# Moving the border offsets out of the one-hot rounds of a token-sorting kernel, with its work lists laid out anew

## The chip, the cores and the metric

The kernel runs on one core of a Trainium2 chip. The time is that of one execution on the device, in microseconds (us); the median of several runs is given. The engines are named as in the profile: PE (TensorE's matmuls), PEld (its weight loads), DVE (VectorE), ACT (ScalarE), POOL (GpSimd) and SP (SyncE, which here only issues transfers).

## The reference

8192 tokens (16 sequences of 512) of 512 features in fp32. Each token gets six vectors of 512, weighed by a softmax `w` of six numbers; a two-layer MLP with a layer norm maps their concatenation back, and the input is added:

```python
h = _ln(x, pw_g[pathway_ids], pw_b[pathway_ids])
h = _ln(h, cp_g[compartment_ids], cp_b[compartment_ids])
t = _ln(x, tm_g[time_steps], tm_b[time_steps])
m = x + _mlp_ln(memory_state, ...)[:, None, :]      # n, r alike
s = _ln(x, ms_g[scale_type], ms_b[scale_type])
cat = jnp.concatenate([w[0] * h, w[1] * t, w[2] * m, w[3] * n, w[4] * r, w[5] * s], axis=-1)
out = x + _mlp_ln(cat, int_W1, int_b1, int_W2, int_b2, int_g, int_be)
```

`_mlp_ln` is `silu(s @ W1 + b1) @ W2 + b2`, normalised. `compartment_ids` and `time_steps` are one list of five values; `scale_type` has the values of a mask. So a token's group, its pair (time step, scale), fixes the tables by which `t` and `s` are scaled, and scaling can be folded into the weights of layer 1 for tokens that are sorted by group.

## The kernel before

**Sorting (up to about 36 us).** The kernel sorts the 8192 tokens by group and sequence. With places counted, it must move token numbers to their new place, and it does so with one-hot matrices: 64 columns in 8 rounds of U = 8 (`one_hots`, L874 to L892). In each round DVE compares for `rows_` (L879) and for m of the 8 columns of `cols_`; ScalarE makes the other columns by a Square and a Relu each (L888, L889); PE adds the 8 products into `pn` (L892). Three buffers take turns, so round k waits for the products of round k - 3. `m` is 6 or 5 by turns.

Between the rounds the loop at L1032 puts small steps on the borders between groups: `place_borders`, `count_rows` and `count_ends` after rounds 0, 1 and 3, and after round 4 `row_places`: two products into `poff` on PE, two copies of it by ScalarE (`off` L945, `total` L946), and two comparisons by POOL (`past`, L948). After the rounds `wx_` is scaled (L1036), and `row_pairs` (L1019) makes three sums of products, `pgc`, of which the third comes from `past`. Ahead of the rounds PE does the first layer of the three conditioning MLPs, `ph`.

**Tiles.** The sorted tokens are worked on in 16 tiles of 512 tokens, each of 4 row groups of 128. A tile's work is cut into some 200 pieces, named by letters, a tile (`p` the previous, `c` the current, `n` the next, `m` the next but one) and a number. Three lists of such names set the order in which all engines' instructions are issued: `ORDER` (startup: conditioning, tables, tile 0, parts of tile 1, extra rows), `WINDOW` (run 15 times with w = 0 to 14) and `LAST`. Within an engine instructions run in this order, and semaphores join the engines. The pieces needed below:

- on PE: `lX`, `lV`, `lH` (`layer1`, L404), `m7` (`half_product`, L452, a half product of layer 1), `q7` (`seventh`, L546, one of seven products by which layer 2 is made, into `pq_0a`, `pq_0b`, `pq_1a`, `pq_1b`);
- layer 1 to layer 2: `ha` adds (DVE, L472), `hs` is the Silu (ScalarE, L475), `tz` turns 32 x 32 blocks (DVE, L197), `sZ` spreads them (transfers issued by SP, `catZ<-rZ`), `zs` makes the sums that the seven products need (POOL, L532 to L538);
- layer 2 out: `kb` puts the bias into a `pq` (ScalarE, L520), `kf` copies a first part (ScalarE, L556, L558), `sf` adds the second to it (DVE, L565), `ku` and `sl` the last ones; `lq` (ScalarE, L612) and `lv` (DVE) make the sums of squares, `lp` the power of them (POOL, L625), `lb` scales, `po` puts out;
- `sp` and `bd` (ScalarE L257, DVE L265) build the scaled weights `vs` of a row group, and run only where the group has a new segment (`if_new`);
- `fs`, `fp`, `fn` (statistics, their power on POOL, norm), `gc`, `gh`, `ga`, `gx`, `gt` (gathers by POOL), and for the conditioning `cs`, `cp` (power on POOL, L1283), `cn`, `ct` (`pt`, PE, L1295).

## Time and profile before

| what | us |
|---|---|
| three runs, lowest / median / highest | 917.75 / 918.54 / 918.93 |
| the profiled execution | 922.05 |
| its span in the profile | 920.3 |

The profiled execution is one execution of its own and longer than the median; its span is 1.75 us shorter than its time, which is what lies around the span.

| engine | busy us | share of the span |
|---|---|---|
| PE | 887.0 | 96% |
| DVE | 726.6 | 79% |
| POOL | 669.5 | 73% |
| ACT | 520.4 | 57% |

A share is a mean over stages. Where the engine with the most work is idle, and what it then waits for, is read stage by stage: from the busy time of every stretch, from the list of its waits, and then from the timeline around a wait, in which a bracket behind an instruction gives the idle time of its engine before it and what ended it.

### The profile page before, as it was taken

The numbers are of one execution on the slowest core, as the hardware profiler recorded it, in microseconds if no ns is written. First come the engines' busy times: TensorE is split into PE (matmuls) and PEld (weight loads), VectorE is DVE, ScalarE is ACT, GpSimd is POOL, SyncE is SP. The second block draws the span as 40 slices with busy tenths as digits, with TensorE's granted clock in tenths as the row PEclk, the third lists the DMA queues.
The fourth block names the chain that finished last, engine by engine and source line by source line (L and its number), as shares of the span: only waits on it lengthen the run. The fifth ranks groups of instructions, "written<-read, shape, count | busy, mean of one in ns | idle before, by whom it ended". The sixth has DMA issues, their size and how long they took to land. (4 is left out here: it accounts for less than half of the span.)

```text
span 920.3 us, 13553 instructions
## 1 busy us (share of the span) xinstructions
PE 887.0 (96%) x3617; PEld 642.2 (70%) x3617; DVE 726.6 (79%) x1360; ACT 520.4 (57%) x1261; POOL 669.5 (73%) x730
## 2 busy tenths in 40 slices
PE   6989899999999999999999999999998999999995
PEld 6744346868686877768686868777685867778682
DVE  8687776868787798968787878869697888879565
ACT  4669835464655648374646556574757466573413
POOL 9777778577778678686868687867767777876452
PEclk9989999999999999999999999999999999999998
DMA  8757686777777777777778686777666776776513
GB/s 273 231 183 228 201 251 186 192 230 197 228 187 233 196 218 192 208 206 208 230 199 222 196 234 183 234 204 214 180 190 198 202 226 187 228 195 192 148 41 111
DMA packets 88557, 185.40 MB, mean 201 GB/s; under 512 B 24324, under 2 KB 24388, under 8 KB 88476
## 3 DMA queue, kind: packets, MB, share of 16 engines
q0 software_dynamic: 31104, 104.88, 40.0%
q1 hardware_dynamic: 56668, 79.53, 29.6%
q8 instruction: 30, 0.49, 0.2%
q14 instruction: 51, 0.42, 0.2%
q10 hardware_dynamic: 704, 0.08, 0.1%
HBM read 100.48 MB, written 19.97 MB: 131 GB/s over the span
## 5 line engine op out<-in xcount | busy, mean ns | idle before, releaser
L404 PE MATMUL p<-vs,catV 128*128 128x512 f32 x512 | 228.1, 593 | 4.0 <-DVE vs L265 1.7
L404 PEld LDWEIGHTS p<-vs,catV 128*128 128x128 f32 x512 | 96.6, 190 | 108.4 <-issue 100.8
L452 PE MATMUL p<-wh__81,catH 128*128 128x256 f32 x480 | 110.9, 379 | 0.0
L452 PEld LDWEIGHTS p<-wh__81,catH 128*128 128x128 f32 x480 | 91.2, 190 | 12.4
L638 POOL DMA_INDIRECT out<-yb,tok x64 | 76.9, 1201 | 31.3 <-issue 15.1
L376 ACT ACTIVATE pw<-pw,rsh 128x512 f32<-128x512 f32 x64 | 45.6, 714 | 92.9 <-DVE pw L383 53.7
L475 ACT ACTIVATE add<-add 128x512 f32<-128x512 f32 x64 | 39.6, 625 | 91.8 <-DVE add L472 72.2
L350 ACT ACTIVATE junk<-pw 128x512 bf16<-128x512 f32 x60 | 37.6, 626 | 88.2 <-DVE pw L347 39.1
L171 POOL DMA_INDIRECT cp<-cp_rows,i_cp x64 | 74.4, 1162 | 14.5 <-issue 12.8
L625 POOL TENSOR_TENSOR rsy<-vey,mhalf 128x4 f32<-128x4 f32 (+1 forms) x16 | 23.6, 1474 | 83.1 <-DVE veh L368 70.1
L391 POOL TENSOR_TENSOR xbs<-xbs,rows 128x512 f32<-128x512 f32 x64 | 82.2, 1286 | 1.3
L171 POOL DMA_INDIRECT xbs<-in_x,tok x64 | 66.0, 1031 | 22.0 <-issue 18.2
L171 POOL DMA_INDIRECT pw<-in_pw,i_pw x64 | 63.0, 984 | 25.1 <-issue 12.2
L171 POOL DMA_INDIRECT add<-rows,i_add x64 | 66.9, 1045 | 19.3 <-issue 19.3
L383 DVE SCALAR_TENSOR_TENSOR pw<-pw,sumsh,cp 128x512 f32<-128x512 f32 x60 | 45.6, 761 | 39.7 <-DMA cp<-cp_rows,i_cp 31.2
L317 ACT ACTIVATE xm<-xbs,nmx,rsx 128x512 f32<-128x512 f32 x64 | 49.0, 807 | 26.9 <-DVE nmx L311 12.5
L372 POOL TENSOR_TENSOR rsh<-veh,mhalf 128x1 f32<-128x1 f32 x64 | 48.5, 758 | 14.9 <-DVE veh L368 11.6
L452 PE MATMUL p<-wt,catH 128*128 128x256 f32 x240 | 56.7, 379 | 0.0
L452 PE MATMUL u<-wt,catX 128*128 128x256 f32 x240 | 56.6, 379 | 0.0
L346 DVE SCALAR_TENSOR_TENSOR pw<-xbs,sums,pw 128x512 f32<-128x512 f32 x60 | 46.0, 767 | 12.5 <-DMA pw<-in_pw,i_pw 6.8
L452 PE MATMUL u<-wx__80,ss 128*128 128x256 f32 x240 | 54.5, 379 | 0.0
L452 PEld LDWEIGHTS u<-wx__80,catX 128*128 128x128 f32 x240 | 45.6, 190 | 12.7 <-issue 6.9
(439 smaller groups left out, 2131.2 us busy)
## 6 DMA issues: line engine op xcount, KB each, us to landing
catX<-rX SPq DMA_DIRECT2D x240, 64.0 KB
catV<-rV SPq DMA_DIRECT2D x240, 64.0 KB
catZ<-rZ SPq DMA_DIRECT2D x240, 64.0 KB
catH<-rH SPq DMA_DIRECT2D x240, 64.0 KB
rows<-adde SPq DMA_DIRECT2D x8, 256.0 KB
yb<-in_int_W SPq DMA_DIRECT2D x1, 1024.0 KB
catH<-in_int_W SPq DMA_DIRECT2D x1, 1024.0 KB
w1x<-in_int_W SPq DMA_DIRECT2D x1, 1024.0 KB
```

The lines of the kernel that those rows point to most:

```text
L171: nc.gpsimd.indirect_dma_start(dst, None, table, bass.IndirectOffsetOnAxis(ap=idx, axis=0), **kw)
L317: nc.scalar.activation(t, st["xb"][:, j, :], AF.Identity, bias=st["nm"][:, j : j + 1], scale=st["rs"][:, j : j + 1])
L346: nc.vector.scalar_tensor_tensor(h, st["xb"][:, j, :], st["sums"][:, 1, j : j + 1], h, ALU.add, ALU.mult)
L350: nc.scalar.activation(junk, x, AF.Identity, accum_out=sums[:, 0, k : k + 1])
L372: nc.gpsimd.tensor_tensor(rs, st.pop(("ve", j)), mhalf[:, :1], ALU.pow)
L376: nc.scalar.mul(pw[:, :D], pw[:, :D], st.pop(("rs", j)))
L383: nc.vector.scalar_tensor_tensor(pw[:, :D], pw[:, :D], st["sh", j][:, 1], cp, ALU.add, ALU.mult)
L391: nc.gpsimd.tensor_add(st["xb"][:, j, :], st["xb"][:, j, :], rows[:, 2, :])
L404: nc.tensor.matmul(st["p1", g], st["c" + blk][:, g, c, :], m[:, c, :], start=(blk == first and c == order[0]), stop=(blk == last and c == ...
L452: nc.tensor.matmul(dst, m[:, c], at_["half1"][k][:, c], start=(k == 1 and c == 0), stop=(c == NC - 1), skip_group_check=True)
L475: nc.scalar.activation(st["add", g], st["add", g], AF.Silu)
L638: nc.gpsimd.indirect_dma_start(out_rows[j], bass.IndirectOffsetOnAxis(ap=tok[:, j, w : w + 1], axis=0), yb[:, j, :], None)
```

## The change

- `row_places` is called behind the eight rounds and not after round 4, and so is `segment_picks`. The two comparisons leave it; they are now `rows_past`, a piece `rp1` of the startup list.
- `row_pairs` makes two sums of products; the third, from `past`, is `rest_rows`, the piece `rp2`, into a buffer `prr` of its own. `past` gets a buffer of its own.
- DVE's number of columns `m` is 5 in five rounds and 6 in three (43 columns, 44 before), ScalarE's 21 (20 before).
- The first layer of the third conditioning MLP (`cond_1(2)`) is issued after round 2 and not ahead of the rounds.
- `ORDER` and `WINDOW` are new; `WINDOW` has the same 197 names. `LAST` is as it was.

```diff
-    for s in range(3):
+    def cond_1(s):
         n = stT[s].shape[1]
...
+    cond_1(0)
+    cond_1(1)
...
-        m = U - 2 - k % 2
+        m = U - 3 + (k % 3 == 2 or k == NQ // U - 1)
...
-    past = [cols[:, n] for n in (3, 4)]
+    past = [t.rearrange("p (v n) -> p v n", v=2)[:, v] for t in (prep.tile([P, 2 * NQ], F32, name="past")[:NB],) for v in range(2)]
...
         nc.scalar.copy(off, poff[:NB, :1])
         nc.scalar.copy(total[:1], poff[:1, 1:2])
+
+    def rows_past():
         for v, i_at in enumerate((i_pos, i_next)):
             pl.tensor_scalar(past[v], i_at[:NB], beg, n_b, ALU.is_gt, ALU.mult)
...
     def row_pairs():
-        pgc = ps.tile([P, 3, Q * NW], F32, tag="p", name="pgc")
+        pgc = ps.tile([P, 2, Q * NW], F32, tag="p", name="pgc")
...
+    def rest_rows():
+        prr = ps.tile([P, Q * NW], F32, tag="p", name="prr")
         for v in range(2):
-            nc.tensor.matmul(pgc[v * NH : (v + 1) * NH, 2], ones[:NB, :NH], past[v], start=True, stop=True)
-        return (pgc,)
+            nc.tensor.matmul(prr[v * NH : (v + 1) * NH], ones[:NB, :NH], past[v], start=True, stop=True)
+        nc.vector.tensor_add(i_rest, i_rest, prr)
...
-        nc.vector.tensor_add(i_rest, i_rest, pgc[:, 2])
...
-        for make in {0: (first_rows, place_borders), 1: (count_rows,), 3: (count_ends,), 4: (row_places, segments, segment_kinds), 6: (segment_picks,)}.get(q0 // U, ()):
+        for make in {0: (first_rows, place_borders), 1: (count_rows,), 3: (count_ends,), 2: (lambda: cond_1(2),), 4: (segments, segment_kinds)}.get(q0 // U, ()):
             make()
+    row_places()
+    segment_picks()
...
-    hs.c.3 bd.n.0 po.p.3
+    m7.c.1.3 sX.n.3
```

**ScalarE in the rounds.** `room` is the scratch of a column, `vs` and `xbs` the buffers of the rounds. Before, around round 4:

```order
L888 ACTIVATE room_118<-room_118,catZ 128x64
L889 ACTIVATE vs_86<-room_118,catZ 128x64
L945 COPY off<-poff 14x1
L946 COPY total<-poff 1x1
L888 ACTIVATE room_118<-room_118,catZ 128x64
L889 ACTIVATE xbs_91<-room_118,catZ 128x64
L888 ACTIVATE room_118<-room_118,catZ 128x64
L889 ACTIVATE xbs_91<-room_118,catZ 128x64
```

After, the last columns and what follows them:

```order
L892 ACTIVATE room_118<-room_118,catZ 128x64
L893 ACTIVATE vs_86<-room_118,catZ 128x64
L892 ACTIVATE room_118<-room_118,catZ 128x64
L893 ACTIVATE vs_86<-room_118,catZ 128x64
L949 COPY off<-poff 14x1
L950 COPY total<-poff 1x1
L1047 ACTIVATE wx__80<-yb,wx 128x2048
```

The copies of `off` and `total` stood between the columns of round 4 and those of round 5, and now stand behind the last column, ahead of `wx_`.

**PE within a window, the second half of layer 2.** `pq_1a` and `pq_1b` are the sums of the second pair of row groups, the `p_` with L404 is `lV.c.2`, and the `p_` with L452 is `m7.c.1.4`. Before:

```order
L546 MATMUL pq_1b<-w_82,catZ 128x256 x2
L546 MATMUL pq_1b<-w2t,zs_5233 128x256 x2
L546 MATMUL pq_1a<-w2t,zs_5233 128x256 x2
L404 MATMUL p_9_2_5306<-vs_85,catV 128x512 x3
L248 UNCONDITIONAL_BRANCH
L404 MATMUL p_9_2_5306<-vs_85,catV 128x512
L248 UNCONDITIONAL_BRANCH
L546 MATMUL pq_1b<-w2t,catZ 128x256 x2
L546 MATMUL pq_1b<-w_82,zs_5233 128x256 x2
```

After:

```order
L546 MATMUL pq_1b<-w2t,zs_5254 128x256 x2
L546 MATMUL pq_1b<-w_82,catZ 128x256 x2
L452 MATMUL p_9_3_5202<-wt_1595,catH 128x256 x4
L546 MATMUL pq_1a<-w2t,zs_5254 128x256 x2
L546 MATMUL pq_1b<-w2t,catZ 128x256
L248 UNCONDITIONAL_BRANCH
L546 MATMUL pq_1b<-w2t,catZ 128x256
L546 MATMUL pq_1b<-w_82,zs_5254 128x256
L248 UNCONDITIONAL_BRANCH
L546 MATMUL pq_1b<-w_82,zs_5254 128x256
L404 MATMUL p_9_2_5329<-vs_85,catV 128x512 x4
```

`lV.c.2` stood ahead of the last two products into `pq_1b` (`q7.p.1.4` and `q7.p.1.3`) and now stands behind them; `m7.c.1.4`, which stood near the end of the window, now stands among them.

**ScalarE at the same place of the window.** L558 with `pq_1b` is `kf.p.3`, L612 is `lq.p.0`, L317 the norm of the next tile's rows. Before:

```order
L520 COPY pq_1b<-rows 128x512
L239 TENSOR_LOAD new_v
L556 COPY yb<-pq_1a 128x256
L317 ACTIVATE xm_1_5311<-xbs_89,nmx,rsx 128x512
L317 ACTIVATE xm_3_5313<-xbs_89,nmx,rsx 128x512
L558 COPY yb<-pq_1b 128x256
L569 COPY yb<-pq_1a 128x256
```

After:

```order
L556 COPY yb<-pq_1a 128x256
L520 COPY pq_1b<-rows 128x512
L317 ACTIVATE xm_1_5314<-xbs_89,nmx,rsx 128x512
L317 ACTIVATE xm_3_5316<-xbs_89,nmx,rsx 128x512
L612 ACTIVATE junk,ssy<-yb 128x512
L558 COPY yb<-pq_1b 128x256
L317 ACTIVATE xm_2_5338<-xbs_89,nmx,rsx 128x512
L317 ACTIVATE xm_0_5340<-xbs_89,nmx,rsx 128x512
L569 COPY yb<-pq_1a 128x256
```

`lq.p.0` now stands ahead of `kf.p.3`; it stood behind it and behind the copy of L569.

## Rows read from the trace of the kernel before

**Rows 1.** The first part of the page.
```profile
span 920.3 us, 13553 instructions
...
PE 887.0 (96%) x3617; PEld 642.2 (70%) x3617; DVE 726.6 (79%) x1360; ACT 520.4 (57%) x1261; POOL 669.5 (73%) x730
```

**Rows 2.** Stretches: length, busy PE, PEld, DVE, ACT, POOL; clock, DMA, GB/s.
```profile
57.00:75.00 18.00, 15.31 (x65) 6.61 (x64) 14.41 (x42) 14.83 (x35) 13.48 (x14) 0.81 0.44 132
...
75.00:165.00 90.00, 85.20 (x253) 44.23 (x252) 63.80 (x117) 59.76 (x134) 68.05 (x67) 1.00 0.74 217
...
165.00:855.00 690.00, 683.01 (x2724) 516.05 (x2723) 568.81 (x1026) 398.42 (x967) 512.82 (x507) 1.00 0.73 207
```

**Rows 3.** Waits of PE: total us, times, longest.
```profile
PE pq_0b L546 <- POOL yb L532: 4.3, 5, 1.6
...
PE p L404 <- DVE vs L265: 1.7, 1, 1.7
```

**Rows 4.** Timeline, 23 to 36 us: start, us, engine, line, work [idle <-releaser].
```profile
23.66 4.02 POOL L948 TENSOR_SCALAR rows<-room,begs,n_b 14x64 f32<-14x64 f32 x2
...
25.11 3.66 PE L892 MATMUL pn<-vs 128*64 128x128 f32 x32
...
28.88 1.52 PE L892 MATMUL pn<-xbs 128*64 128x128 f32 x12
...
28.98 0.15 ACT L945 COPY off<-poff 14x1 f32<-14x1 f32 x1 [4.42 <-PE poff L944]
...
30.68 0.43 PE L892 MATMUL pn<-xbs 128*64 128x128 f32 x2 [0.27 <-ACT xbs L889]
...
31.66 3.87 PE L892 MATMUL pn<-vs 128*64 128x128 f32 x32
...
34.95 1.99 ACT L1036 ACTIVATE wx__80<-yb,wx 128x2048 f32<-128x2048 f32 x1
```

**Rows 5.** Timeline, 57 to 60 us, POOL and PE.
```profile
58.00 0.59 POOL L1283 TENSOR_TENSOR rsc<-vec,mhalf 96x1 f32<-96x1 f32 x1
...
59.48 0.52 PE L1295 MATMUL pt<-ident,room 96*128 96x96 f32 x4 [1.98 <-issue]
```

**Rows 6.** Timeline, 692 to 709 us, ACT, DVE, POOL, PE.
```profile
695.14 2.55 ACT L257 ACTIVATE vs<-ws,scs 128x512 f32<-128x512 f32 x4
...
697.60 0.61 ACT L475 ACTIVATE add<-add 128x512 f32<-128x512 f32 x1
...
698.25 0.71 DVE L197 STREAM_TRANSPOSE rZ<-add 128x512 f32<-128x512 f32 x1 [2.32 <-ACT add L475]
...
708.13 0.73 POOL L532 TENSOR_TENSOR yb<-catZ 128x256 f32<-128x256 f32 x1 [1.75 <-DMA catZ<-rZ]
...
708.91 0.48 PE L546 MATMUL pq_0b<-w2t,yb 128*128 128x256 f32 x1 [1.61 <-POOL yb L532]
```

**Rows 7.** Timeline, 561 to 566 us, ACT, PE, DVE.
```profile
561.58 0.35 ACT L558 COPY yb<-pq_1b 128x256 f32<-128x256 f32 x1
...
561.67 3.60 PE L404 MATMUL p<-vs,catV 128*128 128x512 f32 x8
...
562.70 0.38 DVE L565 TENSOR_TENSOR yb<-yb,pq_1b 128x256 f32<-128x256 f32 x1
...
563.86 0.63 ACT L612 ACTIVATE junk<-yb 128x512 bf16<-128x512 f32 x1
...
564.39 0.19 ACT L612 ACTIVATION_READ_ACCUMULATOR junk<-yb 128x1 f32 x1
...
565.10 1.03 PE L546 MATMUL pq_1b<-w2t,catZ 128*128 128x256 f32 x4
...
565.97 1.03 PE L546 MATMUL pq_1b<-w,zs 128*128 128x256 f32 x4
```

**Rows 8.** The page's costliest groups, L625 on POOL.
```profile
L625 POOL TENSOR_TENSOR rsy<-vey,mhalf 128x4 f32<-128x4 f32 (+1 forms) x16 | 23.6, 1474 | 83.1 <-DVE veh L368 70.1
```

**Rows 9.** Timeline, 642 to 645 us, PE.
```profile
642.84 2.38 PE L404 MATMUL p<-vs,catV 128*128 128x512 f32 x5 [1.70 <-DVE vs L265]
```

73 lines of the change are left out of this document (37 added, 36 removed).

## The prediction

> **What bounds the kernel now.** I read the page's share of busy time first: PE works 887.0 us of a span of 920.3 us [rows 1]. The 33 us left are all that any change of order can win, unless it removes PE work or gives PE a faster clock, so the next thing to see is where they lie. The table by stretches says it [rows 2]: from 165 to 855 us, the steady windows, PE is busy 683.01 of 690 us and idle 7.0; from 75 to 165 it is idle 4.8; from 57 to 75 it is idle 2.7 of 18, and the granted clock there is 0.81, the one stretch of this table in which it is well under 1. The list of PE's waits names most of the windows' idle time [rows 3]: 4.3 us in five waits for POOL's `yb` (the correction that a seventh product of layer 2 reads, L532) and 1.7 us in one for `vs` (L265). These six waits are 6.0 of the 7.0 us.
>
> So a step of the change counts if it shortens PE's work or one of those waits. What it does to ScalarE (57% busy) or POOL (73%) alone costs nothing until PE waits for it.
>
> **The one-hot rounds.** Before, ScalarE stands 4.42 us in the copy of `off`, because the product that it reads is queued on PE behind the 32 matmuls of a round (25.11 us, 3.66 us long) [rows 4]. It is then late with its two columns of the next round: PE idles 0.27 us at 30.68, and the same again (0.28) at 31.39. The 16 matmuls of that half round begin at 28.88 and the next 32 at 31.66, so they take 2.78 us; at the pace of the row at 25.11 (3.66 / 32 = 0.114 us) they would take 1.83. The change puts product and copy behind the last round, so ScalarE isn't held any more: 0.95 us less.
>
> The other edits here. DVE makes 43 columns in place of 44 and ScalarE 21 in place of 20: one more Square and Relu, hidden by the 4.42 us that ScalarE no longer stands. Uncovered it would be two instructions, under 1 us. `cond_1(2)` moves 8 matmuls from ahead of the rounds to behind round 2; the number is the same, so 0. The two products of the third row pair move into a piece of the startup list (`rp2`) with DVE's addition: again the same work, PE's share two short products, 0. POOL's two comparisons (4.02 us at 23.66 [rows 4]) move into the same list behind the table products: POOL is held there in place of here. Queued behind them on POOL are gathers and powers for the extra rows and tile 1, and `rp2` on PE and DVE waits for them; I take 0, since these gathers are issued well ahead of use, and up to +4 if the whole hold reached PE (in the bounds of the next term). `off` is copied ahead of the scaling of `wx_` (34.95), which in before starts before PE's last product of the rounds is done; it now waits for a product queued behind the same matmuls, some 0.6 us later. DVE reads the result of the rounds at the same time, and PE has the products of the cond vectors and tile 0 in its queue, so I take 0. Bounds of the whole term: 0, if DVE's compares and not ScalarE set the pace of rounds 5 to 7, and -2, if the later rounds close up too. Taken: **-0.95**.
>
> **The startup list, behind the rounds.** It is laid out anew in all engines, so its sum is bounded, not added up. The gap of this stretch is one PE wait of 1.98 us, for `pt` at 59.48 [rows 5]. Its operand comes through DVE from POOL's power (L1283), which runs at 58.00, behind gathers of tokens. In the new order the four gathers `gt.0` still stand ahead of `cp`, which comes before `cn` and `ct`: the same chain of the same instructions. So the gap stays, and with it the low clock behind it. Taken: **0**. The bounds: if the gap is closed, the 2.7 us of idle time go and also what the clock takes, (1 - 0.81) x 18 = 3.4 us, together -6.1; if POOL's moved comparisons are uncovered in their new place, +4.
>
> On the clock the row shows this: 0.81 granted in the 18 us in which PE stood 2.7 us, 1.00 in the stretch behind it, in which it was busy 85.2 of 90 [rows 2]. [...]
>
> **The windows.** WINDOW has the same 197 pieces in another order, so PE's busy time stays and only its waits move.
>
> Three of the five `yb` waits are of one kind [rows 6]: ScalarE runs the four `s_part` instructions (L257, 695.14, 2.55 us), needed only when a row group has a new segment, ahead of the last `hidden_silu` (697.60). DVE turns its result at 698.25, SP spreads it, POOL adds at 708.13 after 1.75 us of waiting for that transfer, and PE starts at 708.91 after 1.61 us idle. Two things stand otherwise in the new order: the silu of row group 3 no longer stands behind the whole of the window's last products, since a half product (`m7.c.1.4`; 4 products by the order, which the trace counts as 8 matmuls) is taken out from among them; four of such a size start 0.87 us ahead of the next four (565.10 and 565.97 [rows 7]), so the eight are 1.73 us of PE's time. ScalarE's queue in the next window begins with this silu, then the copies (L520), then L257, in the same order as before. I give the chain 0.55 us of the 1.73, because the silu still waits for DVE's addition and that for the last other products: 3 x 0.55 = 1.65 (bounds 0 and the 4.3 whole).
>
> The other two `yb` waits have POOL late with a power (`fp.c.3`); POOL spends 83.1 us in 16 windows idle ahead of L625 (`lp.p`) [rows 8], 5.2 each, nearly all for DVE's work. The new order issues `gc.n.0` ahead of it, in that idle time, and not between it and the power `fp.n.0`, so what follows on POOL is sooner by about one gather. The two are short, so I take 0.9 off both together (bounds 0 and 4.3 - 1.61 = 2.7).
>
> The wait for `vs`: ScalarE's L257 and then DVE's L265 are late, and PE starts at 642.84 after 1.70 [rows 9]. Same head start: 1.0 (bounds 0 and 1.7).
>
> Against these stands one new tight place. `q7.p.1.4` writes the second `pq_1b` group, and must wait until DVE has added the first (L565), which needs ScalarE's copy of it (L558). Before, PE does the eight products of `lV.c.2` in between (561.67 to 565.10, 3.43 us), and L565 ends at 562.70 + 0.38 = 563.08, 2.0 us ahead of need [rows 7]. In the new order the 3.43 us move behind, `m7.c.1.4` comes in front (1.73), so PE wants `pq_1b` at 561.67 + 1.73 = 563.40, and `lq.p.0` (0.63 at 563.86, and 0.19 for its read-out, 0.82) stands ahead of L558 on ScalarE. The cover falls from 2.0 us to 0.3. In a quiet window that holds; in the five disturbed ones, where DVE and ScalarE run up to a microsecond late, I put 0.2 each: +1.0 (bounds 0 and the second rival below). `kf` and `sf` are behind it on their engines, and the next thing late would be `lV.c.2`.
>
> Windows together: -1.65 - 0.9 - 1.0 + 1.0 = **-2.55**; bounds -6 (all six waits gone) and +6 (0.4 us of new waiting in each of 15 windows). LAST is unchanged: 0.
>
> **Sum.** -0.95 + 0 - 2.55 = -3.5. It is made against the profiled execution, 922.05 us (a span of 920.3 and 1.75 around it): 918.55. The median of the timed runs is 918.54, 3.51 below the profiled one, so the forecast is 918.54 - 3.5 = 915.0.
>
> **The rivals.**
> 1. The gain is eaten. For it: in 57 to 75 us ScalarE is busy 14.83 of 18 us [rows 2], so a start 1 us sooner meets a full engine, and the chain of the silu [rows 6] has SP and a transfer in it that a sooner silu needn't move. Against: the rounds' loss is PE's own. Then 918.54 less 0 to 1: about 918.
> 2. Slower: the wait of `q7.p.1.4` for L565 comes in every window. Its price is 0.3 of missing cover and more when `lq.p.0` (0.82) delays L558 fully, 0.82 - 0.3 = 0.5 to 0.7, say 0.6: 15 x 0.6 = 9.0, so -0.95 - 3.55 + 9.0 = +4.5, 923.0. It decides from (0.95 + 3.55 + 1.84) / 15 = 0.42 us a window. Against it: ScalarE is free 43% of its time [rows 1] and L558 and L565 take 0.73 us together, so part of the 0.82 is taken up.
> 3. The `pt` gap closes after all, because the power comes sooner with fewer pieces between: -6.1 more, 908.9. Against it: four gathers still stand ahead of it on POOL.
>
> **How the numbers follow.** Forecast 0.5 (912 to 917.5), gain eaten 0.2 (917 to 919), slower 0.17 (920 to 926), gap closed 0.13 (906 to 911). Leaving out most of the slower case's upper part and the lowest of the gap case, the range is 908 to 921. What a measurement of this kernel can tell from no change is about 0.2%, 1.84 us, so faster means under 916.7 and slower over 920.4. Faster: 0.13 + 0.9 x 0.5 = 0.58; slower: nearly all of its case, 0.16; the same: the rest, 0.26.
>
> **What would show it.** In the profile after: the copy of `off` with no wait that holds a round, and no idle time of PE in the rounds from 28 to 32; PE's wait for `pt` still near 2 us and a clock of about 0.8 behind it; five or fewer waits of `pq_0b` for `yb` with a sum of 1 to 3 us; a new row "pq_1b waits for DVE" with about 1 us. Wrong it is if that row has 5 us or more, if PE's busy time moves by over 3 us (the clock), or if the startup ends more than 3 us earlier or later: then the list laid out anew decides, which I bounded and did not add up.

## The result: 0.3% slower, and the profile after

The changed kernel takes 923.31 us (median of 16 runs, 920.22 to 926.8). The kernel before, run beside it, takes 920.18 us (16 runs, 917.53 to 922.67). The ratio is 1.0031 with a 95% interval of 1.0016 to 1.0046: slower by 2.9 us, 1.5 to 4.2. The forecast was 915.0, range 908 to 921. It was made on a median of three runs, 918.54; over 16 runs the same kernel has 920.18, so 1.6 us of the distance is the base and the rest the change. One and the same kernel scatters over 5 us between executions; that matters for all that follows.

The profiled execution of the changed kernel took 924.86 us, 2.81 more than that of before, with PE busy 2.8 us longer (page, first part; before in [rows 1]):

```profile
span 922.7 us, 13762 instructions
...
PE 889.8 (96%) x3617; PEld 639.8 (69%) x3617; DVE 724.8 (79%) x1360; ACT 518.6 (56%) x1263; POOL 649.3 (70%) x730
```

The waits of PE over the whole span (total us, times, longest; before in [rows 3]):

```profile
PE pq_1b L546 <- POOL zs L532: 1.8, 1, 1.8
...
PE pq_0b L546 <- POOL yb L532: 1.4, 3, 0.9
...
PE pq_1b L546 <- DVE yb L565: 1.3, 1, 1.3
...
PE p L404 <- DVE vs L265: 0.9, 2, 0.6
```

The waits that the windows were to lose are lower: `yb` 1.4 for 4.3 us, `vs` 0.9 for 1.7. But `zs` and L565 are new, 3.1 us together. The stretches after (start and end, length, busy time of PE, PEld, DVE, ACT and POOL, granted clock, share and GB/s of the transfers; before in [rows 2]):

```profile
36.00:57.00 21.00, 19.94 (x134) 9.38 (x137) 17.82 (x56) 8.17 (x29) 16.82 (x21) 0.75 0.73 237
...
57.00:75.00 18.00, 16.40 (x96) 7.36 (x87) 11.77 (x34) 17.65 (x42) 10.88 (x12) 0.91 0.46 136
...
165.00:855.00 690.00, 683.79 (x2721) 514.44 (x2720) 562.86 (x1023) 395.22 (x965) 492.29 (x507) 1.00 0.72 206
```

Of before, the first of these stretches is not in [rows 2]:

```profile
36.00:57.00 21.00, 21.00 (x198) 10.95 (x197) 15.33 (x53) 12.27 (x36) 15.48 (x20) 0.92 0.76 244
```

From 165 to 855 us PE is busy 683.79 of 690, 0.8 more than before: the windows are even. From the first product of layer 2 to the last first product it is 714.8 us before (148.0 to 862.8) and 714.8 after (150.5 to 865.4). **In these two profiles the 2.4 us by which the span grew are all there at 150 us.** How much of that is the change and how much the two executions is a question that one profile of each can't answer; the table below takes it up.

In the rounds the change did what it says (timeline; start, us, engine, line, work, in brackets the idle time before and what ended it; before in [rows 4]):

```profile
15.56 5.52 PE L896 MATMUL pn<-vs 128*64 128x128 f32 x32 [0.33 <-DVE bi L917]
...
27.29 1.91 PE L896 MATMUL pn<-xbs 128*64 128x128 f32 x16
...
29.12 1.96 PE L896 MATMUL pn<-vs 128*64 128x128 f32 x16
...
31.32 1.96 PE L896 MATMUL pn<-vs 128*64 128x128 f32 x16 [0.24 <-DVE vs L887]
...
33.49 0.15 ACT L949 COPY off<-poff 14x1 f32<-14x1 f32 x1 [4.49 <-PE poff L948]
```

ScalarE still waits 4.49 us for `off`, but nothing of the rounds is queued behind it; the last products run at 1.96 / 16 = 0.123 us each with one wait of 0.24, and the rounds end at 33.28 us in place of 35.52. Behind them this gain no longer shows. The next table has the landmarks of the profiles that have one of the two startup lists unmoved (e6 but for the tables' load): the granted clock from 36 to 60 us, the end of the rounds, PE's first flip of the extra rows (`px`, a transpose by a product with `ident`), the first product of layer 2, and the way between these two. Ratios are to the kernel before, timed on the same chip; those in brackets are of kernels cut short after three windows.

| kernel | lists | clock | rounds end | first flip | layer 2 | flip to layer 2 | ratio |
|---|---|---|---|---|---|---|---|
| before | old | 0.93 | 35.5 | 78.0 | 148.0 | 70.0 | 1 |
| e3_new_window | old startup | 0.72 | 34.6 | 80.0 | 150.8 | 70.9 | 0.9995 |
| e6_tables_last | old | 0.93 | 34.1 | 77.1 | 147.9 | 70.8 | 1.0026 |
| e9_short_before | old | 0.72 | 34.6 | 79.9 | 150.0 | 70.0 | (0.3473) |
| e7_rounds_alone | old, rounds edited | 0.72 | 33.3 | 79.0 | 149.7 | 70.7 | 1.0002 |
| e10_short_rounds | old, rounds edited | 0.86 | 33.4 | 76.2 | 145.8 | 69.5 | (0.3480) |
| e15_rounds_new_window | old startup, rounds edited | 0.72 | 33.4 | 79.2 | 150.6 | 71.4 | 1.0015 |
| e4_new_order | new startup | 0.93 | 35.6 | 79.9 | 152.6 | 72.7 | 1.0009 |
| after | new, rounds edited | 0.72 | 33.3 | 78.0 | 150.5 | 72.6 | 1.0031 |
| e2_old_window | new startup, rounds edited | 1.00 | 33.8 | 77.8 | 149.8 | 72.1 | 1.0015 |
| e14_copy_first | new startup, rounds edited | 0.86 | 33.3 | 78.2 | 150.3 | 72.0 | 1.0020 |
| e11_short_startup | new startup, rounds edited | 0.93 | 33.3 | 76.2 | 149.4 | 73.2 | (0.3498) |

With the startup list of before the last stretch takes 69.5 to 71.4 us in seven profiles, with the new one 72.0 to 73.2 in five; the two do not overlap, whatever the clock did ahead of them. That is not yet a loss: 1.3 us of it is work that the new list puts behind the flip and the old one ahead of it (counted below, under the extra rows' chain). Layer 2 itself begins at 145.8 to 150.8 us with the startup list of before and at 149.4 to 152.6 with the new one, 1.6 us later in the mean, and these ranges overlap. e4's profile is of the longest of its twelve executions (930.01 us).

### The profile page after: what moved, and what is told of

The parts are those of the page before. It is cut to its first block, busy times and chain, and to the rows that moved or that the text cites. A ratio compares the mean times of both kernels' runs of the same rounds, so it can differ in the third digit from the quotient of the medians.

```text
span 922.7 us, 13762 instructions
## 1 busy us (share of the span) xinstructions
PE 889.8 (96%) x3617; PEld 639.8 (69%) x3617; DVE 724.8 (79%) x1360; ACT 518.6 (56%) x1263; POOL 649.3 (70%) x730
## 5 line engine op out<-in xcount | busy, mean ns | idle before, releaser
L404 PE MATMUL p<-vs,catV 128*128 128x512 f32 x512 | 228.3, 593 | 2.8 <-ACTq L248 1.1
L404 PEld LDWEIGHTS p<-vs,catV 128*128 128x128 f32 x512 | 97.0, 190 | 107.2 <-issue 100.4
L452 PE MATMUL p<-wh__81,catH 128*128 128x256 f32 x480 | 111.0, 379 | 0.0
L452 PEld LDWEIGHTS p<-wh__81,catH 128*128 128x128 f32 x480 | 91.4, 190 | 18.2 <-issue 6.7
L171 POOL DMA_INDIRECT pw<-in_pw,i_pw x64 | 67.6, 1057 | 42.4 <-DVE veh L368 27.1
L638 POOL DMA_INDIRECT out<-yb,tok x64 | 66.6, 1040 | 32.4 <-issue 16.4
L171 POOL DMA_INDIRECT xbs<-in_x,tok x64 | 68.2, 1066 | 24.0 <-issue 11.7
L171 POOL DMA_INDIRECT add<-rows,i_add x64 | 69.4, 1084 | 19.9 <-issue 16.2
L171 POOL DMA_INDIRECT cp<-cp_rows,i_cp x64 | 65.4, 1022 | 15.5 <-issue 12.9
L625 POOL TENSOR_TENSOR rsy<-vey,mhalf 128x4 f32<-128x4 f32 (+1 forms) x16 | 19.2, 1202 | 67.6 <-DVE vey L620 67.6
L372 POOL TENSOR_TENSOR rsh<-veh,mhalf 128x1 f32<-128x1 f32 x64 | 44.9, 701 | 30.8 <-DVEq L248 21.6
L317 ACT ACTIVATE xm<-xbs,nmx,rsx 128x512 f32<-128x512 f32 x64 | 48.8, 808 | 21.8 <-DVE nmx L311 21.6
L452 PE MATMUL p<-wt,catH 128*128 128x256 f32 x240 | 56.8, 380 | 0.2 <-DMA catH<-rH 0.2
L452 PE MATMUL u<-wt,catX 128*128 128x256 f32 x240 | 56.6, 380 | 0.1
L452 PE MATMUL u<-wx__80,ss 128*128 128x256 f32 x240 | 54.5, 380 | 0.6 <-DVE veh L368 0.6
L452 PEld LDWEIGHTS u<-wx__80,catX 128*128 128x128 f32 x240 | 45.7, 190 | 12.6 <-issue 3.8
```

What stands on the lines that cost most here:

```text
L171: nc.gpsimd.indirect_dma_start(dst, None, table, bass.IndirectOffsetOnAxis(ap=idx, axis=0), **kw)
L317: nc.scalar.activation(t, st["xb"][:, j, :], AF.Identity, bias=st["nm"][:, j : j + 1], scale=st["rs"][:, j : j + 1])
L372: nc.gpsimd.tensor_tensor(rs, st.pop(("ve", j)), mhalf[:, :1], ALU.pow)
L404: nc.tensor.matmul(st["p1", g], st["c" + blk][:, g, c, :], m[:, c, :], start=(blk == first and c == order[0]), stop=(blk == last and c == ...
L452: nc.tensor.matmul(dst, m[:, c], at_["half1"][k][:, c], start=(k == 1 and c == 0), stop=(c == NC - 1), skip_group_check=True)
L638: nc.gpsimd.indirect_dma_start(out_rows[j], bass.IndirectOffsetOnAxis(ap=tok[:, j, w : w + 1], axis=0), yb[:, j, :], None)
```

## The experiments

### Which of the three parts costs: rounds, startup list, window list

The change has three parts that can be taken apart: the edits of the rounds, `ORDER` and `WINDOW`. Four kernels each had some of them.

**e1_rounds_only**: the edits of the rounds, both lists of before.

```diff
 (before, with all hunks of the change but the two lists)
-    ... nv.e0.2 wh nv.e0.3 ... vv.0.1 ar
+    ... rp1 (13 places ahead of ar) ... vv.0.1 rp2 ar
```

> The kernel before with the edits of the rounds alone: border offsets and copy behind the rounds, 43 and 21 columns, the third conditioning product between the rounds, the third row pair as pieces rp1 (13 places ahead of add_rows in the startup list of before) and rp2 (right ahead of it). Startup list and window list are those of before. Theory A (the rounds gain what the traces show, 35.52 to 33.28 us, and the startup list laid out anew loses it again): last product of the rounds at about 33.3 us, first product of layer 2 (148.0 before) at 146 to 147, time 1.5 to 2.2 us below before, ratio 0.9978. Rival B (startup time is set elsewhere, by clock and transfers, whatever the rounds do): rounds end at 33.3, but layer 2 begins at 148 or later, ratio 1.000.

Measured: 927.94 us, ratio 1.0055 (1.003 to 1.008), above the whole change's ratio, with intervals that meet. The rounds end at 33.4 as expected, the first product of tile 0 comes at 66.9, but layer 2 at 155.7. PE's timeline around the new piece `rp2`:

```profile
79.44 0.48 PE L1035 MATMUL prr<-past,room 14*64 14x64 f32 x4
...
82.90 6.73 PE L404 MATMUL p<-wx__80,catX 128*128 128x512 f32 x8 [2.98 <-ACT catZ L1368]
```

Behind `prr` (L1035) tile 0's third product waits 2.98 us for ScalarE's copy of a flip. All PSUM buffers of this kernel come from one ring of eight (its pool `ps`, bufs=8), so a buffer more shifts every later user onto another predecessor; by the releaser the product here got one that was still being read. The wait is only half of the price: from 78.8 to 89.0 us this execution was granted 0.50, and the product's 8 matmuls took 6.73 us, where they take 3.60 at a granted 1.00 (before, at 78.47; 3.1 more). Wait and clock together, 6.1 us, are about what layer 2 is later than in e7 below (149.7). The old list was made without that buffer. So this run doesn't isolate the rounds; e7 does.

**e2_old_window**, **e3_new_window**, **e4_new_order**: the other combinations.

```diff
 e2 (after):   -WINDOW of after        +WINDOW of before
 e3 (before):  -WINDOW of before       +WINDOW of after
 e4 (before):  -ORDER of before        +ORDER of after, without rp1 and rp2
```

> The changed kernel with the window list of before; rounds and startup list as changed. Theory A (startup list loses 4.7 us, rounds gain 2.2, windows even): layer 2 begins at 150.5 us as in the changed kernel, time 2.5 us over before, ratio 1.0027. Rival C (the window list is what costs): ratio 1.000 or below.

> The kernel before with the new window list alone. Theory A: the windows are even (714.8 us from the first to the last begin of layer 2 in the profile of before, 714.9 in that of the changed kernel), ratio 1.000 with 0.001 either way; waits for yb 1 to 2 us less, the wait for zs or for DVE's L565 1 to 3 us more. Rival C (the window list is what costs): ratio 1.003 or more.

> The kernel before with the new startup list alone (without the pieces rp1 and rp2, which it does not have); rounds and window list as before. Theory A: the rounds end at 35.5 us, layer 2 begins 4 to 5 us later than 148.0, ratio 1.005. Rival B (the startup time is set by clock and transfers, whatever the rounds do): layer 2 begins at about 150.5 as in the changed kernel, ratio 1.0027. Rival C (the window list is what costs): ratio 1.000 or below.

Measured: e2 1.0015 (0.9987 to 1.0042), e3 0.9995 (0.9972 to 1.0019), e4 1.0009 (0.9987 to 1.0031). The window list alone does nothing that can be measured, against rival C, and its waits for `yb` are 2.3 us there; the forecast's -2.55 would be 0.9972, the very end of the interval. The other two lean to the slow side within their intervals; e4's layer 2 at 152.6 us is where theory A had it, its time is not (1.0009 for 1.005). Single runs of a list differ by more than the list: the stretch of the windows was 714.8, 714.6, 710.9 and 718.1 us in four profiles with the old window list (before, e1, e2, e4).

**e7_rounds_alone**: a cleaner form of the rounds, without another PSUM buffer.

```diff
 (before; shortened, without the parts that it shares with the change)
...
-        m = U - 2 - k % 2
+        m = U - 3 + (k % 3 == 2 or k == NQ // U - 1)
...
-    4: (row_places, segments, segment_kinds), 6: (segment_picks,)
+    2: (lambda: cond_1(2),), 4: (rows_past, segments, segment_kinds)
+    row_places(); segment_picks()     # behind the rounds; the third row pair stays in pgc
```

> The kernel before, with both its lists, and of the change only what frees ScalarE in the rounds: offset products, copies and segment_picks behind the rounds, 43 and 21 columns, the third conditioning product after round 2. POOL's comparisons stay after round 4 and the third row pair stays in pgc (in the first run of the rounds the third pair had a PSUM buffer of its own in the old list, and tile 0's third product waited 3.0 us for a buffer). Theory A: rounds end at 33.4 us in place of 35.5, first product of tile 0 at 66 to 67, layer 2 begins at 146.5 to 148, ratio 0.998. Rival B (the startup time is set elsewhere): layer 2 begins at 148 to 151, ratio 1.000.

Measured: 1.0002 (0.9973 to 1.003). The rounds end at 33.3 us and the time is that of before: rival B as far as the interval goes, which is wide enough for the forecast's -0.95 (0.999).

Four profiles with the startup list of before were granted the same clock, 0.72 from 36 to 60 us, and can be set side by side: e3 and e9 without the edit of the rounds, e7 and e15 (below) with it. The rounds end at 34.6 and 34.6 against 33.3 and 33.4 us, the first flip comes at 80.0 and 79.9 against 79.0 and 79.2, layer 2 at 150.8 and 150.0 against 149.7 and 150.6. Of 1.25 us at the end of the rounds 0.85 are left at the flip and 0.25, less than the scatter, at layer 2.

### The startup timed by itself

Since the windows scatter by several us, four kernels were cut short: startup, three windows, the last list (five runs each).

```diff
-    for w in range(NW - 1):
+    for w in range(3):
         run(WINDOW, w)
-    run(LAST, NW - 1)
+    run(LAST, 3)
... (and the two places that ask for the last tile)
```

> The kernel before cut short: after the startup it runs only three windows and then the last list on tile 3; the other twelve tiles are not worked on and their rows of the output are not written. With most of the windows' own scatter out of it, the startup can be timed. Expected from the profile of before: 148.0 to the first layer 2, then 51.7 + 50.0 + 54.6 + 57.5 and 1.75 around the span, about 313.5 us.

> e7_rounds_alone cut short in the same way (old lists, ScalarE freed in the rounds; twelve tiles left out). Theory A (the rounds' 2.2 us reach the end of the startup): 1.5 to 2.2 us below e9_short_before. Rival B (what sets the end of the startup does not start with the rounds): within 0.7 us of it.

> e2_old_window cut short in the same way: rounds and startup list as changed, window list of before (twelve tiles left out). Theory F (the change's 2.9 us are lost in the startup): 2 to 3 us over e9_short_before. Rival G (they are lost in the windows): within 0.7 us of it.

> e11_short_startup with the tables' load lt ahead of lh, cut short in the same way (twelve tiles left out). Theory D (the wait for the tables is what the new startup list loses): 2 us below e11_short_startup. Rival E (something later sets the end, as the full run e5_tables_first had it, with layer 2 at 153.2): within 0.7 us of it, or over it.

Measured: before 320.72 us (319.38 to 321.45), rounds edited 320.61 (317.31 to 322.6), new startup list 322.64 (320.12 to 324.12), with the tables first 321.58 (319.94 to 323.58). As ratios to the full kernel before: 0.3473 (0.3464 to 0.3483), 0.3480 (0.3468 to 0.3491), 0.3498 (0.3488 to 0.3507), 0.3482 (0.3469 to 0.3496). The first was expected at 313.5 us, 7 us too low. The first and the third interval don't meet: rounds and new startup list together are 0.0025 of the full time slower, 2.3 us, most of the change's 2.9, and nothing else differs between these two kernels. The edited rounds with the old lists lie within 0.7 us of before, which points at the startup list, as theory F has it; against the edited rounds alone the intervals meet, though. The full kernels show less of it: 1.4 us in e2 and 0.8 in e4, with intervals that hold 1.

Where in the kernel the 2.3 us arise the traces don't say. In the one profile of each, layer 2 begins at 149.96 us in the short kernel before and at 149.38 with the new list, and what follows takes 167.6 and 169.0 us, with the same lists from there on (169.8 in e10, which has the old lists too).

### The tables behind the big loads

In the changed kernel ScalarE stands 4 us at 50 to 55 us (timeline):

```profile
54.65 0.99 ACT L1250 ACTIVATE room<-room,wx 128x128 f32<-128x128 f32 x3 [4.01 <-DMA room<-in_tm_bT]
...
55.11 1.93 PE L1275 MATMUL pb<-wt,room 128*32 128x512 f32 x8 [0.73 <-ACT room L1250]
...
61.50 0.50 PE L1306 MATMUL pt<-ident,room 96*128 96x96 f32 x4
```

It waits for three small tables (`lt`, moved in packets of 20 and 12 bytes, not of 4 as the expectation of e5 says). The new startup list issues their load behind `lh` (a load of 1 MB) and `lo` on SP's queue: at 43.87 us in place of 37.10. ScalarE's next work is queued behind; from 57 to 75 us it is busy 17.65 of 18 us. PE's `pt` (L1306, L1295 before) no longer waits, but only since PE itself comes 2 us later to it, at 61.50 in place of 59.48 [rows 5]; that alone isn't the list, since e3 and e9 with the old one come to it at 62.1, without a wait too.

```diff
 e5 (after)
-    he.0 eh.2 lh wk.2.1 xe.0 wk.2.0 sz gh.0.0 he.1 g5 lo lt fl.3 ...
+    he.0 eh.2 lt lh wk.2.1 xe.0 wk.2.0 sz gh.0.0 he.1 g5 lo fl.3 ...
 e6 (before)
-    he.2 xt.0.1 lt xs.0.1 ... lh gh.0.0 tt fl.2 xe.0 g5 lo xt.0.2 ...
+    he.2 xt.0.1 xs.0.1 ... lh gh.0.0 fl.2 xe.0 g5 lo lt tt xt.0.2 ...
```

> The changed kernel with one name of its startup list moved: lt (the load of the three small tables, 4-byte pieces) ahead of lh (the 1 MB load of wh_) as it stands in the kernel before; in the changed list it stands behind lh and lo on SP's queue, was issued at 43.87 us (37.10 before), and ScalarE waits 4.01 us for it at 54.65 with sct, catX, the four L257 and the norms queued behind. Theory D (this wait is what makes the new startup list lose the rounds' gain): ScalarE's wait is gone, pt is reached at 58 us in place of 61.5, the first product of tile 0 comes at 66 to 67 in place of 68.9, layer 2 begins at 147 to 149, ratio to the kernel before 0.998 to 1.000. Rival E (something later sets the end of the startup): the wait is gone, but layer 2 begins at 150 to 151 all the same, ratio 1.003.

> The reverse in the kernel before: lt moved behind lh and lo (and tt, its user, behind it). Theory D: ScalarE waits 4 us or more for the tables, the first product of tile 0 comes at 70 in place of 67.9, ratio 1.002 to 1.003. Rival E: the wait appears, but layer 2 begins at 148 to 149, ratio 1.000.

Measured: e5 1.0031 (1.0007 to 1.0054), the changed kernel's own ratio; e6 1.0026 (1.0004 to 1.0048) in time, though its profiled execution was a quick one (918.76 us) with layer 2 at 147.9. In e5 ScalarE has the tables without a wait, and tile 0's first product comes at 66.9 in place of 68.9:

```profile
50.38 0.99 ACT L1250 ACTIVATE room<-room,wx 128x128 f32<-128x128 f32 x3
...
75.69 1.52 ACT L317 ACTIVATE xme<-xbs,nmx,rsx 128x512 f32<-128x512 f32 x2 [2.45 <-POOL rsx L300]
...
77.33 0.63 PE L1361 MATMUL px<-ident,pre 128*128 128x128 f32 x4 [1.89 <-ACT xme L317]
...
79.07 1.09 PE L1361 MATMUL px<-ident,pre 128*128 128x128 f32 x4 [1.11 <-ACT vs L257]
...
79.95 6.08 PE L404 MATMUL p<-wx__80,catX 128*128 128x512 f32 x8
```

But then PE stands 1.89 and 1.11 us ahead of the flips, since their input `xme` is ready at 76 to 77 us as ever: it comes from gathers that POOL issues and that the tables have no part in. Layer 2 began at 153.2. Of that 2.5 us and more are the clock's: this execution was granted 0.50 from 78.1 to 84.9 us, and tile 0's third product took 6.08 us in place of 3.60; e12 lost 1.7 us there in the same way (5.30 us, 0.51 from 79.8 to 83.2). e8 (below) has the same startup list, the same wait of 1.89 us ahead of the flip and 1.00 from 75 to 150 us, and its layer 2 at 150.45 is no sooner than with the tables behind. In e6 the wait came (3.13 us), layer 2 no later than before, yet its time is slower by 0.4 to 4.4 us; no trace here shows why. So theory D isn't borne out by the full kernels: the tables' wait is real and mostly covered. The short one leaves it open: e12's ratio lies midway, 1.5 us under e11's, with intervals that meet.

### The extra rows' chain, 75 to 105 us

The stretch from the first flip to layer 2 that is 2 us longer in the profiles with the new list can be divided at the first product of the extra rows, `pe`. The profiles are those of the table above; times in us, in brackets PE's matmuls:

| startup list | flip to layer 2 | PE busy in it | flip to `pe` | PE busy in it | `pe` to layer 2 |
|---|---|---|---|---|---|
| old, seven profiles | 69.5 to 71.4 | 66.6 to 67.0 (179) | 4.5 to 4.8 | 4.5 to 4.6 | 64.7 to 66.5 |
| new without `rp2` (e4) | 72.7 | 67.6 (183) | 6.4 | 5.0 | 66.4 |
| new, four profiles | 72.0 to 73.2 | 68.2 (187) | 6.6 | 5.5 | 65.4 to 66.6 |

So the difference lies between the flip and `pe`, and half of it there is work: `prr` and four transposes of tile 0 (`ptH`), which the old list has ahead of the flip. The other 1.1 us are two waits. But ahead of the flip PE waits less with the new list, 0.3 to 0.8 us (1.0 in e4), than with the old one, 1.5 in six profiles of seven (0.5 in before). So the landmark compared more work with less, and the waits around the flips are about even: 1.4 to 1.8 us in the four profiles of the new list against 1.5 to 1.7 in the six. ScalarE and PE there in the changed kernel:

```profile
76.33 1.52 ACT L317 ACTIVATE xme<-xbs,nmx,rsx 128x512 f32<-128x512 f32 x2 [1.16 <-POOL rsx L300]
...
77.75 2.54 ACT L257 ACTIVATE vs<-ws,scs 128x512 f32<-128x512 f32 x4
...
77.97 0.63 PE L1361 MATMUL px<-ident,pre 128*128 128x128 f32 x4 [0.77 <-ACT xme L317]
...
79.33 0.63 PE L1361 MATMUL px<-ident,pre 128*128 128x128 f32 x4 [0.74 <-DVE pre L1354]
...
80.82 0.80 ACT L317 ACTIVATE xme<-xbs,nmx,rsx 128x512 f32<-128x512 f32 x1
...
82.75 0.58 ACT L1368 COPY catZ<-px 128x512 f32<-128x512 f32 x1 [0.42 <-ACTq L286]
...
84.57 3.70 PE L1376 MATMUL pe<-ws,catZ 128*128 128x512 f32 x8 [0.33 <-ACT catZ L1368]
```

and ScalarE in e7_rounds_alone, with the startup list of before (its lines are three lower there for the same work):

```profile
77.42 1.52 ACT L317 ACTIVATE xme<-xbs,nmx,rsx 128x512 f32<-128x512 f32 x2
...
79.41 0.81 ACT L317 ACTIVATE xme<-xbs,nmx,rsx 128x512 f32<-128x512 f32 x1 [0.48 <-DMA rows<-rows]
...
82.73 0.56 ACT L1365 COPY catZ<-px 128x512 f32<-128x512 f32 x1
...
85.32 2.56 ACT L257 ACTIVATE vs<-ws,scs 128x512 f32<-128x512 f32 x4 [0.36 <-ACTq L286]
```

The old list has the four L257 of tile 0 behind the norms (L317, `xme`) and the first copy of a flip; the new one has them among the norms. The next kernels moved something there; their expectations take the longer stretch for a loss.

**e13_product_first**, and **e16_short_product**, the same cut short:

```diff
 (after; e16: after with the window list of before, three windows)
-    ... fv.0.1 ey.1 ey.0 xs.e1.1 ro.1 ... gx.1.2 ea.0 lX.0.0 rp2 ...
+    ... fv.0.1 lX.0.0 ey.1 ey.0 xs.e1.1 ro.1 ... gx.1.2 ea.0 rp2 ...
```

> The changed kernel with one product of tile 0 (lX.0.0) moved ahead of the flips of the extra rows ey.1 and ey.0 in the startup list. In every run with the new list the way from the first flip (px) to the first layer 2 takes 72.1 to 73.2 us, in every run with the old list 69.5 to 70.9; in the new one PE waits 1.4 to 1.5 us in the two flips (0.77 and 0.74 in the changed kernel) with only this product behind them. Theory H (the new list asks for the flips before the extra rows are normed): the waits are covered by the product's 3.4 us, first flip to layer 2 takes 69 to 71 us counted from where the product now starts, time 1 to 1.5 us below the changed kernel, ratio to before 1.0015 to 1.002. Rival I (a later chain sets the end, the 1.5 us come back as another wait): ratio 1.003, layer 2 at 150 to 151.

> e11_short_startup (rounds and startup list as changed, window list of before, only three windows; twelve tiles left out) with lX.0.0 ahead of the flips as in e13_product_first. Theory H: 1 to 1.5 us below e11_short_startup, 321.3 us, ratio 0.348 to 0.3485 (e9_short_before 0.3473, e11_short_startup 0.3498). Rival I: ratio 0.3495 or more.

Measured: 1.0043 (1.0018 to 1.0067) and 0.3511 (0.3492 to 0.3529), no gain. The waits of the two flips are gone and come back at the next step, as rival I had it:

```profile
80.29 1.04 PE L1361 MATMUL px<-ident,pre 128*128 128x128 f32 x8
...
82.96 0.58 ACT L1368 COPY catZ<-px 128x512 f32<-128x512 f32 x1 [0.42 <-ACTq L286]
...
84.78 1.55 PE L1376 MATMUL pe<-ws,catZ 128*128 128x512 f32 x3 [2.61 <-ACT catZ L1368]
```

PE waits 2.61 us for the copies of the flips (L1368), which ScalarE makes at about the same time as in the changed kernel (82.96 and 82.75). Layer 2 begins at 152.5 and 151.4.

**e17_scales_later**, and **e18_short_scales**, the same cut short:

```diff
 (after; e18: after with the window list of before, three windows)
-    ... vd.0 nv.e0.0 sp.0.0 fn.0.2 ... fs.0.1 bd.0.0 fv.0.1 ... ez.1 wh gc.0.1 ...
+    ... vd.0 nv.e0.0 fn.0.2 ... fs.0.1 fv.0.1 ... ez.1 sp.0.0 wh gc.0.1 bd.0.0 ...
```

> The changed kernel with one pair of its startup list moved: sp.0.0 (ScalarE's four L257, 2.54 us at 77.75) behind ez.1 and its partner bd.0.0 (DVE's L265, 2.71 us at 81.55) behind gc.0.1, near where the old list has them. In the changed kernel they stand between the norms of the extra rows (xme) and the copies of their flips (catZ, L1368), for which the extra rows' products pe wait; moving a product ahead of the flips only turned their wait into a wait of pe for that copy (2.6 us in e13_product_first). Theory L (the extra rows' chain over ScalarE sets the pace from 75 to 105 us, and these four instructions lengthen it): the copies come 2 us sooner, pe begins at 82 to 83 in place of 84.6, layer 2 at 148 to 149, time 1 to 2 us below the changed kernel, ratio 1.001 to 1.002. Rival M (the gathers of the extra rows set the pace): layer 2 at 150 to 151, ratio 1.003.

> e11_short_startup (rounds and startup list as changed, window list of before, only three windows; twelve tiles left out) with sp.0.0 and bd.0.0 later as in e17_scales_later. Theory L: 1 to 2 us below e11_short_startup, ratio 0.348 to 0.3485 (e9_short_before 0.3473, e11_short_startup 0.3498). Rival M: ratio 0.3495 or more.

Measured: 1.0029 (1.0002 to 1.0055) in full, 0.3480 (0.346 to 0.35) cut short. The traces do a part of what theory L says:

```profile
78.59 0.63 PE L1361 MATMUL px<-ident,pre 128*128 128x128 f32 x4 [1.11 <-DVE pre L1354]
...
79.26 0.59 ACT L1368 COPY catZ<-px 128x512 f32<-128x512 f32 x1 [0.50 <-PE px L1361]
...
80.92 2.56 ACT L257 ACTIVATE vs<-ws,scs 128x512 f32<-128x512 f32 x4
...
83.34 3.60 PE L1376 MATMUL pe<-ws,catZ 128*128 128x512 f32 x8
```

The copies come 3.5 us sooner, but `pe` hardly does: it begins 6.5 us behind the first flip (6.2 cut short), 6.6 in the unmoved profiles, since the second flip now waits 1.11 us for DVE's `pre` (0.74 before the move). Counted from the start, `pe` at 83.3 and 83.6 lies among the unmoved profiles' 82.8 to 84.8. Layer 2 begins at 148.3 (148.6 cut short) against 149.4 to 150.5 in the four profiles of that startup list unmoved, rounds edited. The short kernel's ratio is the one that theory L gave and 1.7 us below e11's, but its interval reaches e11's; the full kernel's is the one that rival M gave. So the sooner layer 2 of both traces makes this pair a candidate for a part of the loss, not by the way that theory L had (a sooner `pe`), and the timing doesn't settle it.

### The windows

**e8_tables_and_bias**: the bias copy `kb.p.3` where it was.

```diff
 (e5_tables_first, window list)
-    ... q7.p.0.3 xs.n.3 kf.p.2 zs.p.6 ... sH.c.1 kb.p.3 sl.p.1 ...
+    ... q7.p.0.3 xs.n.3 kb.p.3 kf.p.2 zs.p.6 ... sH.c.1 sl.p.1 ...
```

> As e5_tables_first, and in the window list the bias copy kb.p.3 ahead of kf.p.2, as in the kernel before: in the changed kernel the first product into pq_1b (now q7.p.1.7) starts right after the copy L520 and every quiet window is 50.05 us in place of 49.99. Theory D: startup as in e5_tables_first, quiet windows 49.99, ratio 0.997 to 0.999. If the 0.06 us come from another wait: quiet windows stay at 50.05 and the ratio is that of e5_tables_first.

Measured: 1.0061 (1.0038 to 1.0084), 0.003 over e5. The quiet windows are not 49.99 us, as hoped, but 50.34 (50.06 in e5, 49.99 before): 0.35 over before, and PE now loses time at the tight place of the forecast (e8's lines are one lower):

```profile
567.10 0.61 ACT L611 ACTIVATE junk<-yb 128x512 bf16<-128x512 f32 x1
...
567.56 1.03 PE L545 MATMUL pq_1a<-w2t,zs 128*128 128x256 f32 x4
...
567.72 0.35 ACT L557 COPY yb<-pq_1b 128x256 f32<-128x256 f32 x1
...
568.25 0.38 DVE L564 TENSOR_TENSOR yb<-yb,pq_1b 128x256 f32<-128x256 f32 x1
...
568.68 1.13 PE L545 MATMUL pq_1b<-w2t,catZ 128*128 128x256 f32 x4
```

`lq.p.0` (L611) runs ahead of `kf.p.3` (L557); the copy ends at 568.07, DVE's addition at 568.63, and PE's next product starts at 568.68, 1.12 us after the one ahead of it in place of 0.87. So the bias copy, 0.6 us of ScalarE moved ahead, was enough to use up the cover. Against e5 that is 0.28 us a window, 4.2 in fifteen; by the ratio the time moved by 2.8, and the two intervals meet.

In the changed kernel itself this happens once, in the window that begins at 756.5 us:

```profile
765.54 0.72 POOL L532 TENSOR_TENSOR zs<-catZ 128x256 f32<-128x256 f32 x1 [3.83 <-DMA catH<-rH]
...
766.32 1.13 PE L546 MATMUL pq_1b<-w2t,zs 128*128 128x256 f32 x4 [1.78 <-POOL zs L532]
...
770.54 0.61 ACT L612 ACTIVATE junk<-yb 128x512 bf16<-128x512 f32 x1
...
771.15 0.35 ACT L558 COPY yb<-pq_1b 128x256 f32<-128x256 f32 x1
...
771.72 0.38 DVE L565 TENSOR_TENSOR yb<-yb,pq_1b 128x256 f32<-128x256 f32 x1
...
772.15 1.13 PE L546 MATMUL pq_1b<-w2t,catZ 128*128 128x256 f32 x4 [1.25 <-DVE yb L565]
```

POOL has waited 3.83 us for a transfer, and the norm's power (L300) is queued behind it; PE loses 1.78 us at once, ScalarE comes late to `lq.p.0` and the copy, and PE loses 1.25 us again.

**e14_copy_first** and **e15_rounds_new_window**:

```diff
 e14 (after), e15 (e7_rounds_alone with the new window list)
-    ... f1.n.0 q7.p.1.7 q7.p.1.5 m7.c.1.4 q7.p.1.6 nv.n.1 nv.n.3 lq.p.0 kf.p.3 ...
+    ... f1.n.0 q7.p.1.5 q7.p.1.7 m7.c.1.4 q7.p.1.6 nv.n.1 nv.n.3 kf.p.3 lq.p.0 ...
```

> The changed kernel with two neighbours of its window list in the order that they had before: kf.p.3 ahead of lq.p.0 on ScalarE, q7.p.1.5 ahead of q7.p.1.7 on PE. This gives DVE's L565 0.6 us more cover before q7.p.1.4 needs it. Theory J (the missing cover costs in disturbed windows): no wait of pq_1b for DVE's L565 (1.3 us in the changed kernel, 0.36 in every quiet window of e8_tables_and_bias), ratio 1 to 2 us below the changed kernel's 1.0031. Rival K (the windows as changed cost nothing): ratio 1.003.

> e7_rounds_alone (ScalarE freed in the rounds, startup list of before) with the window list of e14_copy_first. If the changed kernel's loss is the startup list alone, and its waits for yb (1.4 and 2.3 us in two runs, 2.5 to 5.6 with the old window list) are a gain that stays: rounds 1.4 us and windows 1 to 2 us better than before, ratio 0.997 to 0.9985. If neither shows in the time: ratio 0.9995 to 1.001.

Measured: e14 1.0020 (0.9997 to 1.0044), e15 1.0015 (0.9998 to 1.0032). Quiet windows are 50.01 us and the wait of `pq_1b` for L565 is gone in both; e14's ratio is 1.0 us below the changed kernel's, inside the intervals. Neither J nor K is decided. e15, with the rounds' gain and without the new startup list, is not faster than before. It is the forecast's -3.5 without the startup list: that would be 0.9962, and its interval excludes it. The rounds' gain and the lower waits don't show in any timed kernel.

## Why the prediction was wrong, step by step

The step that failed is the addition: two gains of waits on PE (-0.95 and -2.55) were counted whole at the end of the kernel, and a list laid out anew was counted as 0. In e15 the two gains together came to nothing (1.0015, 0.9998 to 1.0032), and the startup list, with the edited rounds, cost 2.3 us in the short kernels.

- **The rounds** (-0.95). The term was right: the half round that took 2.78 us takes 1.83 (27.29 to 29.12). The rounds of this pair of profiles ended 2.24 us sooner, but the rest isn't ScalarE's wait. Before, they began later and their first 32 products took 6.53 us in place of 5.52:

```profile
17.00 6.53 PE L892 MATMUL pn<-vs 128*64 128x128 f32 x32
```

  `cond_1(2)`, which I put at 0, has its part in the start: its 8 matmuls take 1.06 us behind round 2 (22.75 to 23.81) and took 1.88 ahead of the rounds (15.19 to 17.07), 0.13 and 0.24 us each, both at a granted clock of 1.00. The rounds end at 33.3 to 33.8 us in all fifteen profiles with the edit and at 34.1 to 35.6 in the five without, 1.5 us apart in the mean.
- **That the gain passes on.** This failed first. I let the 0.95 reach the end whole ("the rounds' loss is PE's own"), since PE was busy behind the rounds but for one gap. But at a lower clock a busy time is not the same amount of work: over the same startup list and about the same stretch the changed kernel and e2_old_window show

```profile
33.30:68.90 35.60, 32.94 (x244) 15.23 (x244) 27.19 (x80) 22.40 (x58) 26.78 (x38) 0.81 0.62 190
```

and

```profile
33.80:69.10 35.30, 28.45 (x244) 14.23 (x244) 27.71 (x81) 22.38 (x58) 27.18 (x38) 1.00 0.62 187
```

32.9 us busy at a clock of 0.81, and 28.4 us busy at 1.00, and tile 0's first product begins at 68.9 and at 69.1. The same work filled the waits or left them open, so something other than PE set when it ended in these two; which chain, no run isolates. With the old list and one clock (0.72) two thirds of the gain reach the first flip and next to nothing layer 2. e7 and e10 (1.0002; 0.3480 against 0.3473) show no gain that can be measured; they don't exclude one of the forecast's size.
- **The startup list** (taken 0, bounds -6.1 to +4). It costs about 2 us: 2.3 by the short kernels, with the edited rounds in it. It was within its bounds, but the value taken was wrong, and so was the reason: I followed one wait (`pt`) and took the rest as even. That wait and the clock of 0.81 behind it belonged to the one execution that I had: e3, e9 and e7, with the same list, have no wait for `pt` and were granted 1.00 from 60 to 68 us (0.57 in before). So when the third rival's event came, the wait gone and 0.91 granted from 57 to 75, it needn't be the change's doing, and nothing was gained: the clock was lower in the stretch ahead, 0.75 from 36 to 57 (0.92 before). That the clock's 3.4 us belong to the gap, as the bound of -6.1 and the third rival have it, was my estimate, and no run shows it. Before was granted 0.50 behind the gap, from 60.4 to 67.1 us, but also from 39.9 to 43.2, with PE busy 21.00 of 21.00 us from 36 to 57; the changed kernel was granted 0.50 from 50.1 to 60.2, and PE had been busy without a wait since 39.5.
- **`rp2` at 0.** No wait for its buffer in the new list, but in the old one: e1's 2.98 us, and 3.1 of lower clock behind it. A moved product also moves the ring of buffers, which the sum didn't count.
- **The windows** (-2.55). The waits fell, `yb` and `vs` together from 6.0 to 2.3 us in the changed kernel, more than the 3.55 taken. Over all full profiles it is less clear: 3.0 to 6.9 us in six with the old window list, 2.3 to 5.6 in eight with the new or a variant of it. What took it back in the changed kernel is what the forecast named and priced at +1.0: L565 ahead of `q7.p.1.4`, 1.3 us once, with 1.8 for `zs` in the same window, and 0.06 us in every window, which it didn't name. The second rival's mechanism was one to fear: e8 has it in every window, 0.35 us of the 0.42 from which it was to decide. In the changed kernel it came once, so that the measured 923.3 is near this rival's 923.0 is chance.
- **The sign.** -3.5 forecast, of which rounds and windows came to about 0, and +2 or so for the startup list that was taken as 0. The runs give the sizes only roughly: by the full kernels the parts (e2 1.0015, e3 0.9995) come to less than the whole (1.0031), within their intervals. What in the startup list costs stays open. The pair of e17 may be a part: layer 2 comes 1.1 to 2.2 us sooner in its trace, its full time is 0.2 us below the changed kernel's.
- **The signs named for being wrong.** None of them came: the row of `pq_1b` has 1.3 us (5 named), PE's busy time moved by 2.8 (3 named), the startup by 2.6 (3 named). They were set without knowing the scatter: the startup of the old list alone ends at 147.9 to 150.8 us in three full profiles.

## What to carry to other kernels

A busy engine need not be the bound: PE's 244 matmuls behind the rounds took 32.94 us at a granted 0.81 and 28.45 at 1.00, and the next landmark came at 68.9 and 69.1. Look at the clock beside the busy time, and at whether two executions with different clocks reach the next landmark at the same time. When an order is laid out anew, compare landmarks (the end of a phase, the first product of the next) over several profiles, since here layer 2 began 2 to 3 us apart in profiles with one startup list, as much as the change; count the work between two landmarks before calling a longer way a loss; and cut the kernel short to time one phase without the others' scatter. A piece that looks free (a bias copy, a buffer more) can open a wait elsewhere: e8's 0.35 us in every window, e1's 2.98.
